# Folding the second layer's first norms into its transform, and writing the head weights once

## The chip, the cores and the metric
The kernel runs on one core of one Trainium2 chip. The metric is device time in microseconds of one execution. Engines are called as in the profile: PE (TensorE, matmuls), PEld (its weight loads), DVE (VectorE), ACT (ScalarE), POOL (GpSimd) and SP (SyncE, which here issues DMAs). SPq and ACTq stand for DMA issues on the queues of SP and ACT.

## What is computed
The input is x of shape (4, 48, 48, 128), in float32: B = 4 images, H = 48 rows, W = 128 columns (the reference calls the axis of 128 the channels) and T = 48 tokens. Two residual layers follow each other:

```python
x = x + _L0_conv_ref(_gn(x), ...)      # a selective scan over the image in four directions
x = x + _L1_conv_ref(_gn(x), ...)      # attention built from Fourier layers

def _gn(v, G=32, eps=1e-5):            # GroupNorm, 32 groups of 4 channels
    m = mean(g, axis=(1, 2, 4)); s = var(g, axis=(1, 2, 4))
    return ((g - m) / sqrt(s + eps)).reshape(v.shape)

def _L1_conv_ref(x, ...):
    xa = x.reshape(B * T, 1, H, W)
    xa_n = _inorm(xa, norm_g[0], norm_b[0])            # per token image: mean and variance over H and W
    k, q = spectral convolution of xa_n to half size + skip, 32 heads
    v    = spectral convolution of xa_n at full size + skip, 32 heads
    attn_w = softmax(q k^T / sqrt(d))                  # 48 x 48 per head and image
    out = attn_w v;  projd = spectral convolution over heads + skip
    attention = _inorm(projd + xa)
    m = two more spectral layers with norms and a gelu
    return _inorm(m) + attention
```

So in the second layer x passes two normalizations at its start: GroupNorm (a scale and a shift for each image and group of the 128 channels), then, per image and token, subtraction of a mean over H and W and multiplication by 1 / sqrt(variance + eps), called r below. The spectral convolutions act on the 2-D Fourier transform of that result.

## The kernel before
`layer0` (up to line 617) is the first layer. Its order on the engines is written out by hand by a helper class; every operation of it is recorded under line 50. It ends when the last image is written to a buffer x1 in device memory, at 4213 us of the profile. Then follows `layer1` (from line 643), in which W lies on the 128 partitions and the free axis is (h, image and token), with BT = B * T = 192. From here up to the last strands the program's operations are put in order by the framework's scheduler, so the order on an engine needn't be that of the text; buffers with few copies (`bufs`) set further limits.

The stages of `layer1` that matter here:

1. *Loads and constants* (656 to 744). x is loaded from x1 into `xa` [128, 48, 192], an image at a time, on SP and ACT in turn (line 744). Each image goes to columns b*48 to b*48+47 of every row h, thus in pieces of 192 bytes in SBUF.
2. *Head weights* (749 to 793). The spectral weights of all heads for V and P are combined into `gw`, transposed (`pgt`, line 789), copied to `gtt`, and written to device memory as `dgt` (line 791), repeated 16 times: the destination is [4, 32, 16, 1152] floats, 2304 KB for each of four k.
3. *Weights in two dimensions* (`spectral_weights`, 948 to 979) for the last two layers. w2 is loaded (ACT queue); a row of it is set to zero; then for each of 2 x 8 blocks POOL makes `wih` (line 971) twice, PE multiplies (`psw`, line 976), ACT copies PSUM to `spw` (line 978, one buffer) and SP stores it to `sp_d` (line 979).
4. *GroupNorm* (990 to 999). For each image and each block of 8 rows ACT copies to a dense block `gblk` (line 992) and DVE takes bn_stats of it (line 993); `group_affine` (620) makes scale and shift, `aff`; four DVE operations apply them to `xa` in place (line 999).
5. *The token norm* (`first_norm`, 695). 48 matmuls with a 128 x 128 matrix of 1/(H*W) (`pm_in`, line 699) sum `xa` over w and h; the mean is subtracted in place on DVE and POOL (`xa`, line 706), ACT squares (`sq`, line 708), 48 more matmuls sum these (`pv_in`, line 710), and r (`in_r`) follows.
6. *Transform along W* (`forward_w`, 721). 48 matmuls `pa_x` (line 729) with `fw` [128, 66]; DVE multiplies by r while it empties PSUM (line 730); SP stores to `da_x` (line 731); `load_a2` (736) reads it back with the axes exchanged, as `a2` [96, 33, 192].
7. *Selections* from `a2` for q and k (`psel`, line 1041), after the transposes of `xa` into `xnt` (lines 1023 and 1026; two tiles of [128, 48, 128], tags p0 and p1). Beside this `prepare` (823) loads small weights, most by SP (lines 893 to 946).
8. *Scores and softmax* (1076 to 1170). They also write `dxt` to device memory, the transformed x.
9. *The head stage* (1216 to 1273). For each of 2 pairs of images, 4 k and 3 q: 16 DMAs on SP fill `xrep` (line 1227, two buffers), each with 16 rows of 4608 bytes from `dxt`. At q = 0 also `grep` (line 1235, four buffers, one per group g of 8 heads): one DMA of 576 KB from `dgt` each. For each of the four g, ACT copies `gp` (1242), DVE forms `v` (1244), POOL `v3` (1248), and PE adds to the accumulators `acc` (1252), with the attention weights as the stationary operand. At the end of each k the sums are emptied, combined and transposed (1258 to 1273).
10. *The last strands* (from 1280): the remaining layers, again in an order written by hand.

`small` and `work` are pools with two buffers for each tag. The tag `blk` in `work` is used by the blocks `a_x` of `forward_w` and by `sq` of `first_norm`. DMAs of SP and of ACT carry one of eight completion semaphores in turn.

Of the kernel before, what the change touches and what calls it, by code (L numbers as in the profile page):

```python
# [10 lines left out]
F32 = mybir.dt.float32  # L11
BF16 = mybir.dt.bfloat16
AF = mybir.ActivationFunctionType
ALU = mybir.AluOpType
# [6 lines left out]
BT = B * T  # L21
# [621 lines left out]
def layer1(ctx, tc, io, x1_dram, out):  # L643
# [17 lines left out]
    def everywhere(name, src, n):  # L661
        return load(name, [128, n], src.partition_broadcast(128), nc.scalar)

    ident = load("ident1", [128, 128], io["c_ident"])
    gmat = load("gmat1", [128, 128], io["c_group"])
    fw = load("fw", [128, 66], io["c_FW"])
    fh = load("fh", [96, 96], io["c_FH"])
    fhi = load("fhi", [96, 96], io["c_FHI"])
    ih = load("ih", [96, 96], io["c_IH"])
    eps = const.tile([128, 1], F32, name="eps1")  # L670
    nc.gpsimd.memset(eps, 1e-5)
    mean_m = const.tile([128, 128], F32, name="mean_m")
    nc.gpsimd.memset(mean_m, 1.0 / (H * W))
    n_g = everywhere("n_g", io["L1_norm_g"], 6)
    n_b = everywhere("n_b", io["L1_norm_b"], 6)
    HB = 8


    turn = [0]

    def either():
        turn[0] += 1
        return nc.gpsimd if turn[0] % 3 == 0 else nc.vector

# [6 lines left out]

    def per_image(t, n=HB):
        return t[:, None, :].to_broadcast([128, n, BT])

    def first_norm(psum, work, x):

        pm = psum.tile([128, 512], F32, tag="st", name="pm_in")
        for q in range(H // 2):
            nc.tensor.matmul(pm[:, 0 : 2 * BT], mean_m, x[:, 2 * q : 2 * q + 2], start=(q == 0), stop=(q == H // 2 - 1))  # L699
        m = small.tile([128, BT], F32, tag="in_m", name="in_m")  # L700
        nc.scalar.copy(m, pm[:, 0:BT])
        nc.vector.tensor_add(m, m, pm[:, BT : 2 * BT])
        pv = psum.tile([128, 512], F32, tag="st", name="pv_in")
        for q in range(0, H, HB):
            d = x[:, q : q + HB]
            either().tensor_sub(d, d, per_image(m))
            sq = work.tile([128, HB, BT], F32, tag="blk", name=f"sq_{q}")
            nc.scalar.activation(sq, d, AF.Square)
            for j in range(0, HB, 2):
                nc.tensor.matmul(  # L710
                    pv[:, 0 : 2 * BT], mean_m, sq[:, j : j + 2], start=(q + j == 0), stop=(q + j == H - 2)
                )
        r = small.tile([128, BT], F32, tag="in_r", name="in_r")
        nc.scalar.copy(r, pv[:, 0:BT])
        nc.vector.tensor_add(r, r, pv[:, BT : 2 * BT])
        nc.scalar.activation(r, r, AF.Sqrt, bias=eps)
        nc.vector.reciprocal(r, r)
        nc.vector.tensor_scalar(r, r, n_g[:, 0:1], None, ALU.mult)
        return r

    def forward_w(psum, work, src, r, name):


        da = dram.tile([2, 33, H, BT], F32, name=f"da_{name}")
        for q in range(0, H, HB):
            a = work.tile([66, HB, BT], F32, tag="blk", name=f"a_{name}{q}")
            for j in range(0, HB, 2):
                p = psum.tile([128, 512], F32, tag="mm", name=f"pa_{name}{q}_{j}")
                nc.tensor.matmul(p[0:66, 0 : 2 * BT], fw, src[:, q + j : q + j + 2], start=True, stop=True)
                nc.vector.tensor_mul(  # L730
                    a[:, j : j + 2], p[0:66, 0 : 2 * BT].rearrange("p (a t) -> p a t", t=BT), per_image(r, 2)[0:66]
                )
            nc.sync.dma_start(da.rearrange("c k h t -> (c k) h t")[:, q : q + HB], a)
        return da

# [5 lines left out]

    xa = img.tile([128, H, BT], F32, name="xa")
    for b in range(B):
        dmas[b % 2].dma_start(xa[:, :, b * T : (b + 1) * T], x1_dram[b])

    pair_t = [img.tile([128, H, 128], F32, tag=f"p{p}", name=f"xnt{p}") for p in range(2)]
    sp_d = [dram.tile([96, 32, 96], F32, name=f"sp_d{i}") for i in range(2)]
# [3 lines left out]
    NC = 384  # L751
    dgt = dram.tile([4, NH, 16, 3 * NC], F32, name="dgt")
    with ExitStack() as pw:
# [30 lines left out]
        for k in range(4):  # L784
            gt = q1.tile([NH, 3, NC], F32, name=f"gtt{k}")
            for c in range(3):
                p = ps_t.tile([128, 512], F32, tag="tr", name=f"pgt{k}_{c}")
                for j in range(3):
                    nc.tensor.transpose(p[0:NH, j * 128 : (j + 1) * 128], gw[:, 3 * k + j, c], ident)
                nc.scalar.copy(gt[:, c], p[0:NH, 0:NC])  # L790
            nc.sync.dma_start(
                dgt[k], gt.rearrange("h c n -> h (c n)")[:, None].to_broadcast([NH, 16, 3 * NC])
            )
    ws_q = everywhere("ws_q", io["wQs"].rearrange("h o -> (h o)"), NH)
# [153 lines left out]
    def spectral_weights(psum, work):  # L948
# [3 lines left out]
        for i, m in enumerate((fh, fhi)):  # L952
# [4 lines left out]
            fht.append(t)  # L957
        none = work.tile([1, 2, 1], F32, tag="none", name="none", bufs=1)
        nc.gpsimd.memset(none, 0.0)
        for n in range(2):  # L960
            w2 = work.tile([96, 2, 32], F32, tag="w2", name=f"w2_{n}", bufs=2)
            for c in range(2):
                for i in range(2):
                    nc.scalar.dma_start(w2[i * 48 : (i + 1) * 48, c], io[f"wM{n}"][c])
            for i in range(2):
                nc.scalar.dma_start(w2[48 * i : 48 * i + 1, :, 0:1], none)
            for k0 in range(0, 32, 4):
                p = psum.tile([128, 512], F32, tag="mm", name=f"psw{n}_{k0}")
                for c in range(2):
                    t = work.tile([96, 4, 96], F32, tag="wih", name=f"wih{n}_{k0}_{c}")  # L970
                    nc.gpsimd.tensor_mul(
                        t,
                        ih[:, None].to_broadcast([96, 4, 96]),
                        w2[:, c, k0 : k0 + 4, None].to_broadcast([96, 4, 96]),
                    )
                    nc.tensor.matmul(p[0:96, 0:384], fht[c], t, start=(c == 0), stop=(c == 1))  # L976
                t = work.tile([96, 4, 96], F32, tag="spw", name=f"spw{n}_{k0}", bufs=1)
                nc.scalar.copy(t, p[0:96, 0:384].rearrange("p (k m) -> p k m", m=96))
                nc.sync.dma_start(sp_d[n][:, k0 : k0 + 4], t)


    with ExitStack() as ph:
# [5 lines left out]
        for b in range(B):  # L988
            st = small.tile([128, 6, 6], F32, tag="st", name=f"st1_{b}")
            for q in range(6):  # L990
                blk = small.tile([128, HB, T], F32, tag="gblk", name=f"gblk{b}_{q}")
                nc.scalar.copy(blk, xa[:, q * HB : (q + 1) * HB, b * T : (b + 1) * T])
                nc.vector.bn_stats(st[:, q], blk.rearrange("p a t -> p (a t)"))
            nc.vector.bn_aggr(mv[:, b], st)
        aff = small.tile([128, 2, B], F32, tag="aff", name="aff1")
        group_affine(nc, small, psst, gmat, eps, mv[:, :, 0], mv[:, :, 1], aff[:, 0], aff[:, 1], B, "l1")
        for b in range(B):
            v = xa[:, :, b * T : (b + 1) * T]
            nc.vector.tensor_scalar(v, v, aff[:, 0, b : b + 1], aff[:, 1, b : b + 1], ALU.mult, ALU.add)
        r0 = first_norm(psst, work, xa)  # L1000
        prepare()
        pl = ph.enter_context(tc.tile_pool(name="l1_plain", bufs=1))
        plain = pl.tile([128, 4, 2, BT], F32, name="plain")


        da = forward_w(psum, work, xa, r0, "x")
        a2 = zp.tile([96, 33, BT], F32, tag="z96", name="a2_x")
        load_a2(a2, da, 33)
        b48 = small.tile([128, 1], F32, tag="b48", name="b48")
        nc.vector.tensor_scalar(b48, n_b[:, 0:1], 1.0 / H, None, ALU.mult)  # L1010
# [5 lines left out]
        for p in range(2):  # L1016
            nc.tensor.matmul(pr[0:96, p : p + 1], r0[0:1, p * 96 : p * 96 + 96], one1, start=True, stop=True)
        nc.scalar.copy(r_t, pr[0:96, 0:2])
        for p in range(2):
            for q in range(0, H, 4):  # L1020
                pt = psum.tile([128, 512], F32, tag="mm", name=f"pxn{p}_{q}")
# [158 lines left out]
    with ExitStack() as ph:  # L1180
# [38 lines left out]
        for pair in range(2):  # L1219
            for k in range(4):  # L1220
                acc = [ps_y.tile([128, 512], F32, tag=f"acc{c}", name=f"acc{pair}_{k}_{c}") for c in range(3)]
                gr = []
                for q in range(3):
# [7 lines left out]
                    for g in range(4):  # L1231
                        t = f"{pair}_{k}_{q}_{g}"
                        if q == 0:
                            r = pg.tile([128, 3, NC], F32, tag="grep", name=f"grep{t}")
                            nc.sync.dma_start(
                                r.rearrange("p c n -> p (c n)"),
                                dgt[k, 8 * g : 8 * g + 8].rearrange("h r n -> (h r) n"),
                            )
                            gr.append(r)
# [592 lines left out]
```

## Time and profile before
| what | value |
|---|---|
| median of three runs | 5088.06 us (5079.85 to 5090.88) |
| the profiled execution's own time | 5084.95 us |
| its span | 5083.1 us |
| last write of x1 issued | 4213.1 us |
| first `psel` matmul | 4390.9 us |
| head stage, first `acc` to last | 4547.8 to 4808 us |
| SP in the head stage | 384 `xrep` issues of 72 KB, 32 `grep` issues of 576 KB |
| head weights written | four stores of 2304 KB |

Times in the profile count from the span's start. "Busy" is the time an engine executes; waiting is not counted. A line of the kind `A <- B: t, n, u` in the waits says that A stood idle for t us in n places until B was done. The chain is followed back from the last instruction to whatever released each step. The span's shares are averages over both layers: the first, with 4213 of the 5083 us, sets PE 83%, DVE 83%, POOL 79% and ACT 57%, and says little about the rest. What lies between 4213 and 4810 has to be read window by window.

### The profile page before, as it was taken

To read this page: it belongs to the slowest core of one execution; us is meant where nothing else is said; L and a number is where in the kernel's file an instruction comes from. 1 tells how busy PE (TensorE), PEld (TensorE's weight loads), DVE (VectorE), ACT (ScalarE), POOL (GpSimd) and SP (SyncE) were. 2 spreads that over 40 slices of the span, in tenths; PEclk is the share of its full clock that TensorE was granted. 3 is DMA by queue.
4 is the path that set the end of the run, shared out by engine and by line. 5 is a ranking of instruction groups with operands and counts; after the bars stand their busy time and mean duration, and the time that the engine had idled before them with its cause. 6 is when DMAs were issued, how large, how long until landed. Compare 5 with 4: busy or idle time off the path is not lost. (4 is left out here: it accounts for less than half of the span.)

```text
span 5083.1 us, 44364 instructions
## 1 busy us (share of the span) xinstructions
PE 4214.9 (83%) x12344; PEld 1897.5 (37%) x12344; DVE 4225.4 (83%) x2908; ACT 2911.3 (57%) x6446; POOL 4033.8 (79%) x2219
## 2 busy tenths in 40 slices
PE   6889898888798988887989888878787785888876
PEld 2334333333343333333433333333333332453343
DVE  3689998989899989898999898999999983356536
ACT  3666566666565666665656666656656552223334
POOL 4589998988899989798999898899999872346531
PEclk9989999999899999998999999999899986989977
DMA  1223233323233333232333332333233226236546
GB/s 54 72 88 101 93 113 92 101 91 96 93 107 105 104 93 100 88 99 92 106 103 107 91 102 84 99 105 103 99 104 94 93 71 127 64 81 176 166 99 152
DMA packets 276767, 509.25 MB, mean 100 GB/s; under 512 B 100602, under 2 KB 185434, under 8 KB 276326
## 3 DMA queue, kind: packets, MB, share of 16 engines
q1 hardware_dynamic: 265318, 502.61, 32.8%
q10 hardware_dynamic: 11200, 3.81, 0.5%
q8 instruction: 97, 1.59, 0.1%
q14 instruction: 152, 1.25, 0.1%
HBM read 462.58 MB, written 43.72 MB: 100 GB/s over the span
## 5 line engine op out<-in xcount | busy, mean ns | idle before, releaser
L50 POOL TENSOR_TENSOR hc<-h,cbc 128x960 f32<-128x960 f32 (+1 forms) x1280 | 2719.2, 2140 | 461.9 <-DVE h L50 337.4
L50 DVE TENSOR_TENSOR_SCAN h<-da,carry,db 128x961 f32<-128x961 f32 (+1 forms) x1280 | 2702.3, 2130 | 121.2 <-ACT carry L50 86.8
L50 ACT ACTIVATE da<-dt,a_neg 128x480 f32<-128x480 f32 (+1 forms) x2560 | 1661.2, 649 | 1247.4 <-DVE h L50 1201.6
L50 PE MATMUL yp<-hc,ident 128*128 128x480 f32 (+1 forms) x5120 | 2279.6, 573 | 6.8 <-POOL hc L50 6.6
L50 PEld LDWEIGHTS yp<-hc,ident 128*128 128x128 f32 x5120 | 1008.0, 199 | 1428.5 <-issue 1022.4
L50 DVE TENSOR_TENSOR db<-du,pb 128x960 f32<-128x960 f32 (+1 forms) x960 | 1063.1, 1107 | 210.6 <-PE pb L50 155.5
L50 PE MATMUL pb<-bs,pick 112*128 112x480 bf16 (+1 forms) x960 | 360.6, 376 | 400.9 <-DVE db L50 399.2
L50 POOL TENSOR_TENSOR db<-du,bbc 128x960 f32<-128x960 f32 (+1 forms) x320 | 688.5, 2152 | 0.0
L50 PE MATMUL pc<-pad,cdiag 128*128 128x480 f32 (+1 forms) x630 | 283.2, 561 | 9.0 <-ACT pad L50 9.0
L1248 POOL TENSOR_TENSOR v<-grep,xrep 128x768 f32<-128x768 f32 x96 | 174.2, 1821 | 111.2 <-PE acc L1252 64.0
L50 POOL TENSOR_TENSOR du<-dt,xc 128x480 f32<-128x480 f32 (+1 forms) x160 | 204.9, 1281 | 37.1 <-ACT dt L50 37.1
L1252 PE MATMUL acc<-v,attn_c 128*64 128x384 f32 x1152 | 212.8, 511 | 25.8 <-POOL v L1248 15.8
L1244 DVE TENSOR_TENSOR v<-gp,xrep 128x1536 f32<-128x1536 f32 x96 | 165.3, 1754 | 82.4 <-PE acc L1252 36.2
L50 PE MATMUL px<-xc,w_xp 128*112 128x480 f32 (+1 forms) x320 | 215.6, 761 | 17.0 <-ACT xc L50 13.3
L50 ACT COPY db<-carry 128x1 f32<-128x1 f32 x1280 | 226.0, 177 | 5.4 <-DVE db L50 2.1
L50 PEld LDWEIGHTS <-pick 112*128 112x128 bf16 x960 | 97.9, 102 | 331.8 <-issue 307.6
L50 ACT ACT_TABLE_LOAD x146 | 187.3, 1283 | 25.5 <-PE gv_g L50 13.8
L50 PE MATMUL pd<-xd,w_dt 8*128 8x480 f32 (+1 forms) x320 | 167.9, 605 | 38.6 <-ACT bs L50 24.6
L50 ACT COPY carry<-h 128x2 f32<-128x2 f32 x1024 | 192.7, 188 | 0.0
L50 PEld LDWEIGHTS pc<-pad,cdiag 128*128 128x128 f32 x630 | 121.9, 194 | 142.3 <-issue 114.8
L50 PE MATMUL yp<-y,ident 128*128 128x480 f32 (+1 forms) x240 | 166.4, 823 | 0.2
L1252 PEld LDWEIGHTS acc<-v,attn_c 128*64 128x64 f32 x1152 | 88.2, 141 | 146.6 <-issue 63.4
(367 smaller groups left out, 3183.2 us busy)
## 6 DMA issues: line engine op xcount, KB each, us to landing
cbc<-cd SPq DMA_DIRECT2D x512, 480.0 KB
bbc<-cd SPq DMA_DIRECT2D x256, 240.0 KB
cbc<-cd SPq DMA_DIRECT2D x128, 384.0 KB
xrep<-dxt SPq DMA_DIRECT2D x384, 72.0 KB
grep<-dgt SPq DMA_DIRECT2D x32, 576.0 KB
bbc<-cd SPq DMA_DIRECT2D x64, 192.0 KB
dgt<-gtt SPq DMA_DIRECT2D x4, 2304.0 KB
x<-in_xT SPq DMA_DIRECT2D x16, 288.0 KB
```

The source lines that it names most:

```text
L50: return lambda *args, **kw: self._tc.keep_in_program_order(emit(*args, **kw))
L1244: nc.vector.tensor_mul(v, gp[:, None, :, 0:NC].to_broadcast([128, 2, 2, NC]), x[:, :, 0:2])
L1248: nc.gpsimd.tensor_mul(v3, r[:, 2:3].to_broadcast([128, 2, NC]), x[:, :, 2])
L1252: nc.tensor.matmul(acc[c][64 * b : 64 * b + 64, 0:NC], attn_c[:, 2 * pair + b, g, q], v[:, b, c] if c < 2 else v3[:, b], start=first, stop ...
```

## The change
In the second layer:

- x is loaded image by image into two tiles `x_in` (dense, two images each), on the tags p0 and p1 that `xnt` uses later. The loads stand ahead of those of `gmat`, `fw` and the head weights; the eight loads of w2 stand ahead of them and are held in constants.
- bn_stats reads `x_in`; the copies to `gblk` are gone. The affine isn't applied to x any more. Its scale multiplies `fw` (`fwa`, one for each image), its shift comes as a bias `fwb` when PSUM is emptied, half on DVE and half on ACT.
- The mean over H and W is summed from `x_in` by 24 matmuls with the scale as weights, image b into partitions 32b to 32b+31 (four column groups); a helper `spread` reduces over h and distributes it to all partitions by small matmuls. The variance is summed the same way. Centring (DVE, from `x_in` into `xa`) and squares (ACT) take one image and 8 rows at a time, 24 operations each.
- The transform doesn't contain mean and r: the mean is taken out of `a2` at frequency 0 (`p0_x`), and `a2` is multiplied by r there, in three DVE operations. `forward_w` and the variance pass are generators that run in turns, and `da_x` is stored on ACT's queue.
- `spectral_weights` sets the row to zero by a multiplication; `wih` is made on POOL for c = 0 and on DVE for c = 1; `spw` has two buffers, and `sp_d` is stored on ACT's queue.
- `dgt` is written once (144 KB for each k), and `grep` is read with eight DMAs of 72 KB, each of which reads one head's row for 16 partitions.

The diff, cut to its core:

```diff
+    x_in = [img.tile([128, 2, H, T], F32, tag=f"p{p}", name=f"x_in{p}") for p in range(2)]
+    for b in range(B):
+        dmas[b % 2].dma_start(x_in[b // 2][:, b % 2], x1_dram[b])
-    xa = img.tile([128, H, BT], F32, name="xa")
-    for b in range(B):
-        dmas[b % 2].dma_start(xa[:, :, b * T : (b + 1) * T], x1_dram[b])
...
     def first_norm
-        for q in range(H // 2):
-            nc.tensor.matmul(pm[:, 0 : 2 * BT], mean_m, x[:, 2 * q : 2 * q + 2], ...)
+        nc.vector.tensor_scalar(a_m, aff[:, 0], 1.0 / (H * W), None, ALU.mult)
+        def sums(p, what, weight):
+            for q in range(0, H, HB):
+                for b in range(B):
+                    nc.tensor.matmul(p[32 * b : 32 * b + 32, 0 : HB * T], weight(b), what(b, q), ...)
+        def spread(p, name, more=False):
+            nc.vector.tensor_reduce(v, p[:, 0 : HB * T].rearrange("p (h t) -> p t h", t=T), AX.X, ALU.add)
+            for b in range(B):
+                nc.tensor.matmul(ob, g_of[:, b], v, start=True, stop=not more)
+                if more:
+                    nc.tensor.matmul(ob, aff[:, 1, b : b + 1].to_broadcast([128, 128]), over_w, ...)
...
-            either().tensor_sub(d, d, per_image(m))
-            nc.scalar.activation(sq, d, AF.Square)
-            for j in range(0, HB, 2):
-                nc.tensor.matmul(pv[:, 0 : 2 * BT], mean_m, sq[:, j : j + 2], ...)
+            for b in range(B):
+                nc.vector.scalar_tensor_tensor(d, x[b // 2][:, b % 2, q : q + HB], aff[:, 0, b : b + 1],
+                    m[:, b, None, :].to_broadcast([128, HB, T]), ALU.mult, ALU.add)
+                nc.scalar.activation(sq[:, b], d, AF.Square)
+                nc.tensor.matmul(pv[32 * b : 32 * b + 32, 0 : HB * T], mean_m, sq[:, b], ...)
+            yield
...
     def forward_w
+            nc.vector.tensor_scalar(fwa[:, b], fw, aff[:, 0, b : b + 1], None, ALU.mult)
+        nc.tensor.matmul(pb[0:66, 0:B], fw, aff[:, 1], start=True, stop=True)
-                nc.tensor.matmul(p[0:66, 0 : 2 * BT], fw, src[:, q + j : q + j + 2], ...)
-                nc.vector.tensor_mul(a[:, j : j + 2], p[0:66, 0 : 2 * BT]..., per_image(r, 2)[0:66])
-            nc.sync.dma_start(da...[:, q : q + HB], a)
+                nc.tensor.matmul(p[0:66, 0 : HB * T], fwa[:, b], x[b // 2][:, b % 2, q : q + HB], ...)
+                if b % 2:
+                    nc.scalar.activation(o, v, AF.Identity, bias=fwb[:, b : b + 1])
+                else:
+                    nc.vector.tensor_scalar(o, v, fwb[:, b : b + 1], None, ALU.add)
+            nc.scalar.dma_start(da...[:, q : q + HB], a)
+            yield
...
-    dgt = dram.tile([4, NH, 16, 3 * NC], F32, name="dgt")
+    dgt = dram.tile([4, NH, 3 * NC], F32, name="dgt")
-            nc.sync.dma_start(dgt[k], gt...[:, None].to_broadcast([NH, 16, 3 * NC]))
+            nc.sync.dma_start(dgt[k], gt.rearrange("h c n -> h (c n)"))
...
     def spectral_weights
-                    nc.gpsimd.tensor_mul(t, ih..., w2[:, c, k0 : k0 + 4, None]...)
+                    (nc.gpsimd, nc.vector)[c].tensor_mul(t, ih..., w2[:, c, k0 : k0 + 4, None]...)
-                t = work.tile([96, 4, 96], F32, tag="spw", name=f"spw{n}_{k0}", bufs=1)
+                t = work.tile([96, 4, 96], F32, tag="spw", name=f"spw{n}_{k0}", bufs=2)
-                nc.sync.dma_start(sp_d[n][:, k0 : k0 + 4], t)
+                nc.scalar.dma_start(sp_d[n][:, k0 : k0 + 4], t)
...
-                blk = small.tile([128, HB, T], F32, tag="gblk", name=f"gblk{b}_{q}")
-                nc.scalar.copy(blk, xa[:, q * HB : (q + 1) * HB, b * T : (b + 1) * T])
-                nc.vector.bn_stats(st[:, q], blk.rearrange("p a t -> p (a t)"))
+                v = x_in[b // 2][:, b % 2, q * HB : (q + 1) * HB]
+                nc.vector.bn_stats(st[:, q], v.rearrange("p h t -> p (h t)"))
-        for b in range(B):
-            v = xa[:, :, b * T : (b + 1) * T]
-            nc.vector.tensor_scalar(v, v, aff[:, 0, b : b + 1], aff[:, 1, b : b + 1], ALU.mult, ALU.add)
-        r0 = first_norm(psst, work, xa)
+        norm = first_norm(psst, work, x_in, aff, xa)
+        trans = forward_w(psum, work, x_in, aff, "x")
+        next(norm)
+        for _ in range(6):
+            next(trans)
+            next(norm)
+        da = next(trans)
+        r0 = next(norm)
...
+        nc.tensor.matmul(p0[0:H, 0:BT], over_h, a2[0:H, 0], start=True, stop=True)
+        nc.vector.tensor_sub(a2[0:H, 0], a2[0:H, 0], p0[0:H, 0:BT])
+        for s in range(0, 33, 11):
+            v = a2[:, s : s + 11]
+            nc.vector.tensor_mul(v, v, r0[0:96, None, :].to_broadcast([96, 11, BT]))
...
-                            nc.sync.dma_start(r..., dgt[k, 8 * g : 8 * g + 8].rearrange("h r n -> (h r) n"))
+                            for i in range(8):
+                                nc.sync.dma_start(r[16 * i : 16 * i + 16]..., dgt[k, 8 * g + i].partition_broadcast(16))
```

## The prediction, made before the changed kernel ran
> **What bounds the kernel now.** I read the windows first, stage by stage, because the page's shares are dominated by the first layer, which the change doesn't touch (its last line is at 4213 us). The columns are the window, its length, busy PE, PEld, DVE, ACT and POOL with instruction counts, granted TensorE clock, DMA share and GB/s.
> ```profile
> 4206.00:4230.00 24.00, 6.65 (x11) 2.74 (x10) 5.40 (x13) 0.00 (x0) 11.95 (x64) 0.57 0.77 146
> 4256.00:4290.00 34.00, 24.55 (x64) 12.56 (x62) 8.40 (x14) 2.26 (x4) 5.56 (x7) 0.79 0.98 201
> 4316.00:4346.00 30.00, 23.27 (x50) 8.17 (x49) 2.79 (x8) 5.88 (x14) 17.81 (x22) 0.80 0.22 62
> 4547.00:4810.00 263.00, 222.24 (x1213) 94.55 (x1212) 174.96 (x118) 84.80 (x117) 170.61 (x94) 0.96 0.57 164
> ```
> From 4206 to 4391 no engine is full and the limiter changes every 30 us; in the head stage (last row) PE leads, with DMA at 164 GB/s. Next the chain of waits between 4205 and 4400 (start, duration, what):
> ```profile
> 4219.79 22.39 DMA xa<-x
> ...
> 4266.30 5.66 DVE xa L999 x4
> 4272.01 18.12 PE pm_in L699 x48
> 4290.89 6.67 DVE xa L706 x2
> 4297.58 1.49 ACT sq L708
> 4299.12 13.18 PE pv_in L710 x40
> ...
> 4316.77 1.87 DMA sp_d<-spw
> 4318.72 0.48 ACT spw L978
> 4319.22 1.88 DMA sp_d<-spw
> ```
> The pair sp_d/spw repeats up to 4346: one spw buffer, so each round is a 0.48 copy and a 1.87 store, and about 30 us go to it while PE holds the following pa_x behind psw. Last, SP's own queue in the head stage (timeline: start, us, line, how many):
> ```profile
> 4538.27 33.33 SPq L1227 DMA_DIRECT2D xrep<-dxt  x48
> 4571.70 1.78 SPq L1235 DMA_DIRECT2D grep<-dgt  x4
> 4573.57 29.26 SPq L1227 DMA_DIRECT2D xrep<-dxt  x48
> 4602.95 2.78 SPq L1235 DMA_DIRECT2D grep<-dgt  x4
> 4605.84 29.52 SPq L1227 DMA_DIRECT2D xrep<-dxt  x48
> ```
> One (pair, k) is 48 + 4 issues; eight of them run from 4538 to 4808, 33.5 us each. The waits view has beside it:
> ```profile
> POOL v L1248 <- DMA xrep<-dxt: 33.4, 8, 18.4
> DVE v L1244 <- DMA xrep<-dxt: 29.7, 9, 7.1
> ```
> so v already waits for xrep eight or nine times, once per k. Taken one by one, issues that queue without a wait start every 0.463 us (0.42 busy and a gap), xrep like grep; the 16-way broadcasts of mask and wpv ahead of them have the same 0.42 and 0.47, so an eighth of the bytes will not be issued faster.
>
> **What the Trainium skill says.** "DMA: Bandwidth & Descriptors", section "Issuing engines are not separate DMA queues", holds that issuing from another engine saves sequencer time and adds no bandwidth: the trace agrees that here the sequencer is the scarce part (0.463 us an issue, while DMA is 57% busy). "TensorEngine Tiling (Array Packing)", Key Properties, says that narrow tiles run side by side and that a change of tile mode drains TensorE; psel at L1041, in four groups of 32 columns, agrees with the first half (163 matmuls of 0.329 us are busy 8.0 us together); the second is shown by no stretch of this trace. "SBUF — State Buffer", section "SBUF: two separate sides", describes a port pair that VectorE and GpSimd lock against each other: L706 takes 4.98 us on POOL and up to 5.01 on DVE against 1.76 undisturbed.
>
> **The change part by part, up to psel** (it starts at 4390.9 now).
> *Load of x.* 3072-byte packets become 9216-byte ones. xrep's 4608-byte packets at 251 ns give 16 x 4608 / 251 = 294 GB/s; 4.72 MB then need 16 us, so x lands near 4236 rather than 4242: 6 gained (0 to 8). The eight small w2 loads now ahead of it run during the first layer's tail.
> *Statistics.* Now 24 copies (0.51 us, ACT) and 24 bn_stats (0.55, DVE) alternate, and bn_stats are kept back by head-weight work; the affine factors come at 4266.3, 24 us after the load. Between the last aggregate (4257.7) and gm_l (4262.4) PE ran psw; that goes. After the last image: 6 x 0.55 + 0.3 + group affine (2 matmul pairs, 1.28 table load, seven small DVE operations: 4.0 + 0.3) plus 1.74 of d_qk and a wQ load that stand in front, 12.5 us: 4248.7. The four affines of 1.47 (5.66 on the chain) are gone. So pm_in may start at 4249 instead of 4272: 23 gained.
> *Means.* 24 matmuls of 384 columns instead of 48. But the scheduled order puts nine of them first and the other fifteen one to one between the 32 psw, which now all precede pa_x. Per k0 two psw and one pm, 3 x 0.65 = 1.95 us; 4249 + 9 x 0.5 + 16 x 1.95 + about 3 of mode changes = 4288. The psw/spw rounds no longer limit (two buffers: (0.48 + 1.9 + 0.3) / 2 = 1.3 a round). That uses up most of the 23 gained (pm_in ended at 4290.1), but psw's 30 us between pr and pa_x vanish.
> *Variance and transform, interleaved.* The blk tag has two buffers, and the order a, sq, a, sq gives a always the same one: a round is 1.2 of evacuation plus the da_x store (3.46 and 3.75 in the chain), 4.8; six rounds 29 us. The engines need less per round: DVE 4 x 0.55 centring (estimate from 128x384 rows) + 2 x 0.55, 3.3; ACT 4 x 0.45 + 2 x 0.5 + one issue, 3.3; PE 8 x 0.65 at most, 5.2, if column groups don't overlap. End 4317; r0, which follows pv, is by then ready. Now centring, squares, pv, psw and pa_x take 4290 to 4367.
> *Spectrum.* p0_x needs the first piece of a2 (load now 8.26 for all, first piece about 3): 4320. xnt's 24 evacuations of 0.683 then take 16.4: psel near 4337 to 4338. The three products with r0 (2.4 each, an estimate: v's 1.76 for 1536 columns, scaled to 2112) end near 4332 and are covered by xnt; without that cover they cost 7.2.
> Sum: 4390.9 - 4338 = **53 us gained**. Bounds: 42 (PE at half clock through a third of the psw loop, 10 more) to 60 (column groups overlap, load at full rate). The single dgt store (576 KB in all in place of 9.4 MB between 4247 and 4294) frees DMA, which nothing above waits for.
>
> **Between psel and the head stage** PE, ACT, DVE and POOL have the same order as before; no change.
>
> **Head stage.** xrep's 48 issues per (pair, k) stay; grep's four become 32 of 72 KB. All on SP: 80 x 0.463 = 37.0 us for each k, where the period is 33.5. So SP, which had 52 x 0.463 = 24.1 us of work and slack, becomes the bound: at least 8 x 3.5 = 28 lost. It doesn't reach this floor, since xrep has two buffers and SP is in order. Once v of (k, 1) has freed a buffer, SP issues 16 for (k+1, 0), then 32 grep, then 16 for (k+1, 1): 64 x 0.463 = 29.6, landing about 2.3 later, then the four v (8.1, PE's acc being 2.2 a group) before the next buffer is free: 40.0 a period, +6.5. Counted the same way the present kernel gives (16 + 4 + 16) x 0.463 + 2.3 + 8.1 = 27, which isn't binding, and PE sets 33.5. Behind the grep run wait (k+1, 1)'s xrep, thus v on DVE and POOL, thus acc on PE, which idles about 6 us a period and may fall to the lower clock (acc 3.6 to 3.9 instead of 2.2), up to 1.7 more. Seven periods x 6.5 (to 7.9) + 7 for the first k: 52 (52 to 62); if part of a grep run is absorbed in slack, the floor of 28. I take **54 lost**. At a pitch of 0.42 (the busy time of an issue alone) the same sum gives 64 x 0.42 + 10.4 = 37.3, 3.8 x 7 + 4 = 31; at 0.36 (the median of grep's 32 present issues, most of which had waited first) 33.4: nothing lost.
>
> **Sum.** -53 + 54 = +1 on 5084.95 (the span of 5083.1 and 1.9 around it). The profile lies 3.1 below the median of the runs, so +1 on 5088.06: **5089**. The tail strands after the head move as a block.
>
> **Rivals.**
> *Head transfers stay hidden.* For: DMA moves 164 GB/s with room, grep's present issues show a median of 0.36 us, and four grep buffers let early ones go ahead. Against: back-to-back issues show 0.463 without exception in shape. Pays from a pitch near 0.40 downward; then -53 + 0 to 20: about 5044 (5033 to 5068).
> *SP's queue outweighs the front (the slower side).* Place: the 32 grep issues between the xrep of (k+1, 0) and (k+1, 1). Price 6.5 a period as above plus the lower clock, 7.9, and PE's restart at every step: up to 66, against a front gain of 42: +15 to +30, about 5110. Decides from a pitch of 0.463 with the lower clock in every k, or a front gain under 45.
> *The front gives less.* psw and pm_in at the lower clock need 3.85 us a k0, +30, and mode changes add; gain 25: 5088 - 25 + 54 = 5117. For: window 4230 to 4256 shows a clock of 0.57. Against: the loop is dense and the clock is 0.79 to 0.9 once PE is busy. I count it with the previous one.
> That the edits don't do what they say: the grep tiles are the same bytes, and the order of issues shows 256 in place of 32, so no.
>
> **How the numbers follow.** Balance (5074 to 5102): 0.46. Transfers hidden: 0.27. SP outweighs or the front gives less: 0.27. 0.2%, about 10 us, is what can be told from no change. In the balance case a quarter each lies beyond 10 us on either side, so faster 0.27 + 0.11 = 0.38, slower 0.27 + 0.12 = 0.39, the rest 0.23. For 8 in 10 the range must reach well into both outer cases: 5048 to 5118; the likeliest one's own is 5074 to 5102.
>
> **What would show it.** Right: psel starting 53 us earlier; no stretch of sp_d/spw pairs; in the head stage SP rows of 32 grep of about 15 us each, a period near 40, v waiting for xrep 6 us more per k, PE busy down from 85% to 72%. Wrong: a period near 33.5 (pitch below 0.40), or psel gaining under 42 with psw or da_x stores on the chain.

## The result and the profile after
The changed kernel takes 5127.2 us (median of four runs; 5124.6 to 5133.5) against 5086.8 beside it. The ratio on record is 1.0092, 95% interval 1.0079 to 1.0104; the two medians alone give 1.0079. It is 40 us slower by the medians, outside the range that was given (5048 to 5118).

The two profiled executions (spans 5083.1 and 5126.9) divide into four stretches. The times are those of the first `psel` matmul and of the first and last `acc` matmul in each trace:

| stretch | before | after | difference |
|---|---|---|---|
| start to first `psel` | 4390.8 | 4350.0 | -40.8 |
| first `psel` to first `acc` | 156.9 | 156.9 | 0 |
| first to last `acc` (the head stage) | 260.8 | 347.8 | +87.0 |
| last `acc` to the end | 274.6 | 272.3 | -2.3 |

So the front did gain, 41 instead of 53, and the head stage lost 87 instead of 54. The timeline of SP's queue in the head stage of the changed kernel (start, us, line, number of issues):

```profile
4511.72 29.50 SPq L1296 DMA_DIRECT2D xrep<-dxt  x48
4541.32 15.32 SPq L1305 DMA_DIRECT2D grep<-dgt  x32
4556.90 29.62 SPq L1296 DMA_DIRECT2D xrep<-dxt  x48
4586.63 14.69 SPq L1305 DMA_DIRECT2D grep<-dgt  x32
```

Between two runs of grep lie 45.3 us here; the eight ends of k are 44.4 apart on the mean, and were 33.5 apart before. POOL in the same k (timeline: start, us of the group, line, and in brackets the idle time ahead of it and what ended it):

```profile
4548.28 1.81 POOL L1318 TENSOR_TENSOR v<-grep,xrep 128x768 f32<-128x768 f32 x1 [6.19 <-DMA grep<-dgt]
4552.42 1.81 POOL L1318 TENSOR_TENSOR v<-grep,xrep 128x768 f32<-128x768 f32 x1 [2.34 <-DMA grep<-dgt]
4556.53 1.81 POOL L1318 TENSOR_TENSOR v<-grep,xrep 128x768 f32<-128x768 f32 x1 [2.30 <-DMA grep<-dgt]
4560.64 1.81 POOL L1318 TENSOR_TENSOR v<-grep,xrep 128x768 f32<-128x768 f32 x1 [2.30 <-DMA xrep<-dxt]
4568.91 3.58 POOL L1318 TENSOR_TENSOR v<-grep,xrep 128x768 f32<-128x768 f32 x2 [6.45 <-DMA xrep<-dxt]
```

The four v of (k, 0) come 4.1 us apart, each held by a landing (eight issues at 0.463 would be 3.7), and v of (k, 1) then waits for the xrep issued behind the last grep. Afterwards (4568.9 to 4587) POOL and PE are busy with v of (k, 1) and (k, 2) until the next run of grep. The windows show the same as an average (length, busy PE, PEld, DVE, ACT and POOL, granted clock, DMA share, GB/s): the second row is the stretch with the grep run, the third the end of the k.

```profile
4507.00:4855.00 348.00, 240.62 (x1208) 96.40 (x1208) 178.46 (x118) 86.74 (x119) 172.45 (x95) 0.85 0.72 129
4541.00:4570.00 29.00, 15.05 (x76) 5.23 (x72) 10.49 (x9) 6.17 (x9) 9.41 (x6) 0.84 1.04 147
4578.00:4587.00 9.00, 8.91 (x56) 4.09 (x54) 7.18 (x5) 2.41 (x3) 7.94 (x5) 1.00 0.44 123
```

PE is busy 69% of the stage (240.6 of 348) where it was 85%. One thing in the second row was not in the prediction: DMA is full (1.04) at only 147 GB/s. The first window below is of the kernel before while grep was loaded, where 290 GB/s passed at a share of 0.94. The other two are of the changed kernel, when xrep alone goes out, just before the grep run and 8 us after it:

```profile
4671.30:4676.20 4.90, 4.90 (x29) 2.89 (x27) 3.15 (x2) 0.00 (x0) 3.72 (x3) 0.85 0.94 290
4536.00:4540.00 4.00, 4.00 (x24) 2.05 (x24) 2.86 (x3) 0.80 (x1) 3.50 (x2) 1.00 0.52 152
4565.00:4573.00 8.00, 2.23 (x8) 1.07 (x10) 3.42 (x2) 1.47 (x2) 3.58 (x2) 0.66 1.04 154
```

The same DMAs pass at the same rate with a share of 0.52 and of 1.04, so a full share alone doesn't show that 147 GB/s is a limit. But SP's queue also waits for landings in the head stage (waiting line, what ended the wait: us in total, times, longest):

```profile
SPq L1296 <- DMA xrep<-dxt: 11.6, 60, 0.4
SPq L1296 <- DMA grep<-dgt: 5.7, 31, 0.2
SPq L1305 <- DMA grep<-dgt: 3.6, 19, 0.3
```

These are 20.9 us, 2.6 for each k. So besides SP's issues there is a second suspect, the transfers themselves, and the experiments had to separate the two.

In the front, the chain of waits of the changed kernel:

```profile
4266.23 1.46 PE psw L1032 x4
4267.69 0.76 PE pm_in L716 x2
4268.45 1.46 PE psw L1032 x4
...
4304.55 3.46 DMA da_x<-a_x
...
4326.05 12.56 DMA a_x<-da_x
4338.73 1.03 DVE a_x L1075
```

The pairs of spw and sp_d are gone. Every 2.22 us PE issues two psw and one pm_in (1.46 + 0.76; each of these float32 matmuls has two records), and nothing else holds the loop. Behind it two da_x stores stand on the chain, this one and one of 4.17 us at 4315.2.

### The profile page after: what moved, and what is told of

Read it like the earlier page. It is cut to its first block, busy times and chain, and to the rows that moved or that the text cites. A ratio compares the mean times of both kernels' runs of the same rounds, so it can differ in the third digit from the quotient of the medians.

```text
span 5126.9 us, 44853 instructions
## 1 busy us (share of the span) xinstructions
PE 4209.6 (82%) x12372; PEld 1882.8 (37%) x12372; DVE 4229.5 (82%) x2945; ACT 2910.8 (57%) x6451; POOL 4011.9 (78%) x2207
## 5 line engine op out<-in xcount | busy, mean ns | idle before, releaser
L1322 PE MATMUL acc<-v,attn_c 128*64 128x384 f32 x1152 | 230.3, 552 | 93.5 <-POOL v L1318 90.9
L1312 ACT COPY gp<-grep 128x768 f32<-128x768 f32 x96 | 76.5, 803 | 193.9 <-DVE v L1314 120.3
```

The lines of the kernel that those rows point to most:

```text
L1312: nc.scalar.copy(gp[:, :, 0:NC], r[:, 0:2])
L1322: nc.tensor.matmul(acc[c][64 * b : 64 * b + 64, 0:NC], attn_c[:, 2 * pair + b, g, q], v[:, b, c] if c < 2 else v3[:, b], start=first, stop ...
```

## The experiments
All ratios are to the kernel before, timed beside it. "Period" is the mean distance of the eight ends of k (the copies of the first accumulator). Period and first `psel` come from the one profiled execution of each kernel.

| kernel | ratio (95% interval) | first `psel` | period |
|---|---|---|---|
| before | 1 | 4390.8 | 33.5 |
| changed | 1.0092 (1.0079 to 1.0104) | 4350.0 | 44.4 |
| head_undone | 1.0001 (0.9992 to 1.0010) | 4388.0 | 33.9 |
| one_issue | 1.0110 (1.0094 to 1.0125) | 4353.2 | 45.3 |
| eight_rep | 1.0171 (1.0156 to 1.0187) | 4392.6 | 44.9 |
| grep_act | 1.0199 (1.0184 to 1.0214) | 4352.5 | 50.8 |
| two_copies | 0.9988 (0.9980 to 0.9996) | 4353.9 | 37.0 |
| wide_8 | 1.0163 (1.0148 to 1.0178) | 4355.6 | 49.2 |
| before_two | 1.0030 (1.0018 to 1.0041) | 4374.5 | 39.0 |
| blk_apart | 0.9982 (0.9975 to 0.9988) | 4351.1 | 37.9 |
| issues_only | 1.0166 (1.0149 to 1.0184) | 4386.0 | 44.2 |
| four_copies | 0.9938 (0.9923 to 0.9953) | 4352.0 | 33.7 |
| four_psw | 0.9911 (0.9896 to 0.9925) | 4345.3 | 33.5 |
| late_16 | 1.0022 (1.0015 to 1.0029) | 4356.2 | 32.9 |

**head_undone**: the changed kernel with the head weights as before.

```diff
+    dgt = dram.tile([4, NH, 16, 3 * NC], F32, name="dgt")
+            nc.sync.dma_start(dgt[k], gt...[:, None].to_broadcast([NH, 16, 3 * NC]))
+                            nc.sync.dma_start(r..., dgt[k, 8 * g : 8 * g + 8].rearrange("h r n -> (h r) n"))
```

> The changed kernel with its head stage as before: dgt written 16 times, grep read by one DMA of 576 KB for each g. Theory A (the 32 grep issues on SP stand between two fills of xrep and lengthen every k): the head's period falls from 44.6 to 33.5 us, 8 x 11 = 88 us, so 5127 - 88 = about 5040 and a ratio to the kernel before of 0.991; psel starts where it does in the changed kernel (4350) or up to 4 us later, since 9.4 MB more are written. Theory C (the front of the layer is what lost, and its gain of 41 us is given back before the head stage): no less than 5085.

Measured: 5084.5, the time of the kernel before. The head's period is back to 33.9, but psel is back too, at 4388.0. The theory was right about the head and wrong about the front: 38 of the front's 41 us go with the store of dgt. SP's timeline and the chain of this kernel show how.

```profile
4241.17 63.80 SPq L852 DMA_DIRECT2D dgt<-gtt  x4
4307.73 34.82 SPq L954 DMA_DIRECT2D w_wK<-in_wK  x7
...
4347.95 4.36 SPq L960 DMA_DIRECT2D w_wK<-in_wK  x15
...
4365.49 0.33 SPq L806 DMA_DIRECT2D a_x<-da_x  x1
```

```profile
4267.84 11.46 DMA sp_d<-spw
...
4297.43 10.28 DMA da_x<-a_x
...
4309.63 11.83 DMA da_x<-a_x
...
4342.71 27.63 issue
4370.34 0.86 PE p_x L1073 x2
```

Four stores of 2304 KB occupy SP from 4241 to 4305. The stores of sp_d and da_x, 1.9 and 3.5 us otherwise, take 10 to 12 us beside them. Then the small weight loads, which stand behind dgt on SP, are late, and SP's part of the load of a2 stands behind these: it starts at 4365.5, against 4325.4 in the changed kernel. The chain has 27.6 us of "issue" up to 4370.3, in which the profile names nothing that PE waits for; that queue fits it. Whether the bytes of the store or its place on SP's queue cost more was not separated.

**one_issue**: dgt written once, one DMA for each grep that repeats each head's row 16 times.

```diff
-                            for i in range(8):
-                                nc.sync.dma_start(r[16 * i : 16 * i + 16]..., dgt[k, 8 * g + i].partition_broadcast(16))
+                            nc.sync.dma_start(r..., dgt[k, 8 * g : 8 * g + 8][:, None].to_broadcast([8, 16, 3 * NC]))
```

> The changed kernel, dgt written once, but grep read by one DMA for each g whose source repeats each head's row 16 times (32 issues in all, the same bytes read from the same rows as in the changed kernel). Theory A (issues): period 33.5, about 5040, like the kernel with the head undone. Theory B (16 partitions that read the same 4608 bytes are slow as a transfer, which also makes the landing of 4.3 us): v still waits for grep, the period stays at 40 or more, 5095 to 5127.

Measured: 5139.6 and a period of 45.3, with 32 grep issues in all. It was a miss for theory A as the only cause. In the k of the window below, POOL's v of (k, 0) come 4.1 to 4.7 us apart, each waiting for its grep: 576 KB (590 thousand bytes) in 4.65 us, 127 GB/s. Columns as above:

```profile
4589.00:4607.00 18.00, 9.10 (x36) 3.75 (x38) 5.65 (x4) 3.36 (x5) 5.42 (x3) 0.62 0.58 137
```

DMA is slow while it is hardly more than half busy (a share of 0.58). That agrees with the Trainium skill, "DMA: Bandwidth & Descriptors", section "Why a DMA increments its semaphore by 16 and not by 1", which says that a DMA goes to as many engines, at most 16, as divide the slowest dimension of both its access patterns: 8 rows lead here, so 8 engines of the 16. The slow landings hold xrep too. The wait of SP's queue for grep in the head stage (us in total, times, longest):

```profile
SPq L1296 <- DMA grep<-dgt: 112.3, 29, 4.7
```

In this k SP issues four grep and four xrep, and the next four xrep go out only 4.1 to 4.8 us apart (4593.9, 4598.7, 4603.4, 4607.5), as the greps land. That fits the eight semaphores that SP's DMAs carry in turn: the ninth DMA waits for the first. So this run takes the issues away and puts landings in their place, at the same point of the queue. It doesn't show what the changed kernel would do if its issues were free.

**eight_rep**: dgt repeated 16 times, grep still read by eight DMAs.

```diff
+    dgt = dram.tile([4, NH, 16, 3 * NC], F32, name="dgt")
-                                    dgt[k, 8 * g + i].partition_broadcast(16),
+                                    dgt[k, 8 * g + i],
```

> The changed kernel, with dgt written 16 times as before, but grep still read with eight DMAs of 72 KB, each of 16 different rows. Theory A (issues): the 256 issues remain, so 5127 within 6 us, period 44 to 45. Theory B (reads of one row by 16 partitions): these are gone, so the period falls by a good part, to 34 to 40, 5045 to 5090.

Measured: 5169.5. The period stays at 44.9, so reading one row 16 times isn't what makes the changed kernel's head slow. (The other 42 us are the front: psel at 4392.6, about as in head_undone.) The transfers are as slow as there with 16 different rows: DMA share 1.04 at 141 GB/s in the grep run.

**grep_act**: the changed kernel's 256 grep DMAs on ACT's queue.

```diff
-                                nc.sync.dma_start(
+                                nc.scalar.dma_start(
                                     r[16 * i : 16 * i + 16]..., dgt[k, 8 * g + i].partition_broadcast(16),
```

> The changed kernel with grep's 256 DMAs issued on ACT's queue instead of SP's; all transfers are the same. Theory A (SP's queue): SP is back to 48 issues a period; ACT has 9.6 us of gp copies and 32 x 0.46 = 15 us of issues in a period of 33.5 and holds them, though gp of one k stands behind grep issues that wait for a buffer; 5040 to 5065. Theory B (transfers): no change, 5115 to 5130.

Measured: 5187.1, period 50.8, slower than on SP. ACT's timeline:

```profile
4613.40 0.80 ACT L1312 COPY gp<-grep 128x768 f32<-128x768 f32 x1 [0.77 <-DMA grep<-dgt]
4613.43 5.63 ACTq L1305 DMA_DIRECT2D grep<-dgt  x8
4621.76 0.80 ACT L1312 COPY gp<-grep 128x768 f32<-128x768 f32 x1 [7.55 <-DMA grep<-dgt]
4621.77 6.85 ACTq L1305 DMA_DIRECT2D grep<-dgt  x8
4630.48 0.80 ACT L1312 COPY gp<-grep 128x768 f32<-128x768 f32 x1 [7.92 <-DMA grep<-dgt]
```

gp of one group stands between the issues of the next: the copy waits for its grep to land, and the next eight issues wait for the copy. One group costs 8.4 to 8.7 us in place of 4.1. That is a chain of its own, so this run doesn't decide between issues and transfers.

**two_copies**: dgt written twice, so that 16 rows stand at the head of the source.

```diff
+    dgt = dram.tile([4, NH, 2, 3 * NC], F32, name="dgt")
+                            nc.sync.dma_start(r..., dgt[k, 8 * g : 8 * g + 8].rearrange("h r n -> (h r) n")[:, None]
+                                .to_broadcast([16, 8, 3 * NC]))
```

> The changed kernel, dgt written in two copies (288 KB for each k), grep read by one DMA for each g whose source is 16 rows (8 heads times 2 copies), each repeated 8 times. Theory D (what is slow is not the number of issues but how a DMA spreads: eight rows at its head keep it on 8 DMA engines[...]): now [...]grep's packets return to about 180 ns, the head period to 33.5, and psel stays near 4351: about 5042, ratio 0.992. Theory B (reads of one row by several packets are slow whatever the spread): the period stays over 40, 5100 to 5135.

Measured: 5074.4; psel 4353.9, period 37.0. Neither theory's number. The windows of a grep load in this kernel and in four_copies (below):

```profile
4612.00:4621.00 9.00, 3.70 (x20) 1.56 (x19) 4.84 (x5) 3.26 (x5) 4.34 (x3) 0.82 1.02 231
```

```profile
4606.00:4612.00 6.00, 4.58 (x31) 2.37 (x28) 3.29 (x4) 0.48 (x1) 4.12 (x4) 1.00 0.95 337
```

With DMA full in both, 231 GB/s pass with two copies and 337 with four. So repeated reading of the same rows does slow a large transfer (the median packet of 4608 bytes takes 322 ns in the window with two copies, 178 in the one with four, and 178 in the kernel before with sixteen). The wait of SP's queue for grep follows suit, here in two_copies and in four_copies:

```profile
SPq L1298 <- DMA grep<-dgt: 55.1, 25, 3.2
SPq L1298 <- DMA grep<-dgt: 25.2, 15, 2.8
```

In the kernel before it is 24.7 us.

**wide_8**: two copies, each grep cut into eight DMAs of 144 columns over all partitions.

```diff
+                            for i in range(8):
+                                nc.sync.dma_start(r...[:, 144 * i : 144 * i + 144],
+                                    dgt[...][:, None, 144 * i : 144 * i + 144].to_broadcast([16, 8, 144]))
```

> As the kernel with two copies, but each grep cut in eight DMAs of 144 columns over all 128 partitions: 256 issues of 72 KB again, now with wide targets. Theory A alone (SP's issues, 0.463 us each): 64 issues in the chain, 29.6 + 2.3 + 8.1 = 40 a period, 5084 + 0 to 10. Theory D alone (transfers): the period returns to 33.5 and the time to 5040 to 5060. If both must be paid as in the changed kernel: 5127.

Measured: 5164.8, period 49.2. A run of 32 such issues takes at least 20.4 us, 0.64 each instead of 0.463, so the run is not the clean test that was meant. With its own pitch the chain of the prediction gives 7.4 + 20.4 + 7.4 + 2.3 + 8.1 = 45.6, 3.6 less than measured.

**before_two**: the kernel before, with dgt and grep of two_copies only.

> The kernel before with only the head weights changed: dgt in two copies, grep by one DMA for each g as in the kernel with two copies. Theory E (the front's gain is a joint one: both the new front and the small store are needed; the 16-fold store keeps SP's queue and the DMA engines, but the kernel before then waits for its chain of spw and sp_d and for the norm anyway): psel from 4391 to 4380 to 4388, 5075 to 5083. Theory F (the store alone held the front; the other edits are worth little): psel near 4355, about 5045.

Measured: 5096.0, with psel at 4374.5, between the two theories. The small store alone gives the old front 16 us, the new front alone (head_undone) gives 3, both give 37 (two_copies) to 41. The gain is joint. The total is no better than before, since grep with two copies costs 41 us in the head stage (301.5 us from first to last acc, against 260.8).

**blk_apart**: two_copies with a tag of its own for the squares.

```diff
-            sq = work.tile([128, B, HB, T], F32, tag="blk", name=f"sq_{q}")
+            sq = work.tile([128, B, HB, T], F32, tag="sq", name=f"sq_{q}")
```

> The kernel with two copies, and the squares on a tag of their own, so that a_x and sq have two buffers each. The rounds of a_x and sq from 4289 to 4325 took 36 us where 29 had been reckoned. If the shared blk buffers make them (a evacuation waits for the store of a_x two blocks back): 6 to 10 us less than the kernel with two copies. If the engines or the da_x stores do: within 3 us of it.

Measured: 5072.4, psel 2.8 us earlier: by the number, within the bound for "not the buffers". The trace says otherwise of the rounds themselves: from the first da_x store to the last they take 21.5 us (4296.3 to 4317.8) instead of 26.7 (4296.6 to 4323.3), so the shared buffers did make them longer. psel gets little of it, because SP, in another order here, is at the small weight loads until 4324 and sends three of its four a2 loads only from 4332.9 on (from 4326.9 with two copies).

**issues_only**: head_undone, with seven tiny DMAs behind each of its four grep DMAs, into a tile that nothing reads.

```diff
+                            for i in range(7):
+                                j = 4 * (((pair * 4 + k) * 4 + g) * 7 + i)
+                                nc.sync.dma_start(junk[:, j : j + 4], dgt[k, 8 * g + i, 0, 0:4].partition_broadcast(16))
```

> The kernel with the head undone (16 copies, one grep DMA for each g) with seven more DMAs behind each grep, of 16 bytes for each of 16 partitions, into a tile that nothing reads: 32 issues for grep again, and hardly a byte more to move. It is compared with the kernel with the head undone (5084, period 33.4). Theory A (issues in the chain xrep, grep run, xrep): 29.6 + 2.3 + 8.1 = 40.0 a period, up to 41.7, so 5084 + 8 x 6.6 to 8.3 = 5137 to 5151. Theory D (only the transfers): period 33.5, 5084 to 5090.

Measured: 5164.5 against 5084.5 for head_undone, 80 us for 224 issues that move 57 KB together. The period is 44.2. SP's timeline:

```profile
4588.55 0.34 SPq L1307 DMA_DIRECT2D grep<-dgt  x1
4588.93 3.20 SPq L1313 DMA_DIRECT2D junk<-dgt  x7
4592.39 28.24 SPq L1299 DMA_DIRECT2D xrep<-dxt  x48
4620.73 0.35 SPq L1307 DMA_DIRECT2D grep<-dgt  x1
```

and POOL's:

```profile
4592.48 1.81 POOL L1325 TENSOR_TENSOR v<-grep,xrep 128x768 f32<-128x768 f32 x1 [2.03 <-DMA grep<-dgt]
4602.45 3.59 POOL L1325 TENSOR_TENSOR v<-grep,xrep 128x768 f32<-128x768 f32 x2 [8.16 <-DMA xrep<-dxt]
4608.62 1.82 POOL L1325 TENSOR_TENSOR v<-grep,xrep 128x768 f32<-128x768 f32 x1 [2.58 <-PE acc L1329]
```

Seven issues in 3.20 us are 0.46 each although they carry 256 bytes. The grep run ends, xrep of (k, 1) goes out, and v starts after 8.2 us without work (6.5 in the changed kernel). The period is longer than even theory A had it (40.0 to 41.7). So issues that carry almost nothing are enough for the changed kernel's longer period. That its transfers cost nothing isn't shown by this: 32 x 72 KB at 147 GB/s are 16.0 us (an estimate), as long as the 15.3 of the issues, and the two run at the same time. No run has the changed kernel's transfers without its issues.

**four_copies**: as two_copies, with `4` copies and a source of [32, 4, 3 * NC].

> As the kernel with two copies, with four (576 KB written for each k, grep's source 32 rows repeated 4 times). If the repeated reading of one row is what keeps grep at 225 GB/s and 330 ns a packet (two copies; 16 copies: 178 ns): packets of 220 to 270 ns, period 34 to 35 in place of 36.0, so 8 to 16 us off in the head stage, and 1 to 4 us on in the front for the larger store: 5060 to 5070. If the number of copies is nothing to it: 5074 to 5078.

Measured: 5050.7. The period is 33.7, psel 4352.0: 38.8 of the front's 40.8 without the loss of the head. That is better than expected; SP waits for grep as little as in the kernel before (25.2 us against 24.7).

**four_psw**: four_copies, with the weights in two dimensions behind the variance pass.

```diff
-        spectral_weights(psum, work)
         mv = small.tile([128, B, 2], F32, tag="mv", name="mv1")
...
         r0 = next(norm)
+        spectral_weights(psum, work)
         prepare()
```

> The kernel with four copies, and the weights in two dimensions (psw and its stores) put behind the variance pass. In the changed kernel 15 of the 24 pm_in matmuls stand singly between psw at 0.76 us each, where four together take 0.85. If that and the wait for a2 (5 us before p0_x, which psw now fills) are real costs of the front: psel 10 to 14 us earlier than with four copies, and the time too. If psw only moves: within 3 us of it.

Measured: 5037.7, 13 us less than four_copies, but psel comes only 6.7 earlier, between the two expectations. Another 4.5 lie between psel and the first acc (156.9 against 161.4); their cause is open. The order on PE in the changed kernel and in this one:

```profile
4257.27 1.53 PE L1032 MATMUL psw<-wih,fht 96*96 96x384 f32 x4
4258.73 0.83 PE L716 MATMUL pm_in<-x_in,a_m 128*32 128x384 f32 x2
4259.49 1.53 PE L1032 MATMUL psw<-wih,fht 96*96 96x384 f32 x4
```

```profile
4251.64 4.33 PE L716 MATMUL pm_in<-x_in,a_m 128*32 128x384 f32 x46
```

The 24 pm_in of the program leave 48 records, two each. Singly, one pm_in takes 0.76 us; here 23 of them, four column groups side by side, take 4.33, or 0.19 each. psw now stands behind the variance pass (4292 to 4325), where the chain has 4.8 us of wih on POOL and a store of sp_d of 5.9, which gives part of it back.

**late_16**: dgt written once, copied to 16 copies in device memory beside the scores.

```diff
                     nc.sync.dma_start(dxt[b, k], xt.rearrange("r c n -> r (c n)"))
+                    if b == 0:
+                        nc.sync.dma_start(dgt16[k], dgt[k][:, None].to_broadcast([NH, 16, 3 * NC]))
```

> The changed kernel, dgt written once in the front and copied 16-fold from device memory to device memory beside the scores, where DMA is 13 to 16% busy; grep as in the kernel before. If the front's gain needs only that the 9.4 MB stay out of it, and the head needs 16 copies: psel near 4355 (one of the four copies is issued ahead of the a2 load), period 33.5, 5045 to 5055. If the copies collide with dxt's stores in the scores, these get longer by their waits: 5060 to 5090.

Measured: 5093.7, above both expectations. psel (4356.2) and the period (32.9) came as wanted, but the first acc came 193 us after psel instead of 157: six dxt stores go out between 4501 and 4537, after the scores, and xrep needs them. Whether the copies held them by their traffic or the scheduler by another order was not separated.

## Why the prediction was wrong
Two terms of its sum were off. The head's loss was put at 54 and was 87; the front's gain was put at 53 and was 41. The first is the larger, and it is the step that failed: the period with 32 grep issues was mis-sized. One sentence on dgt was also wrong in kind. Of the signs that the prediction had named for being right, the grep runs of about 15 us, the vanished pairs of sp_d and spw and PE's fall (69%; 72% forecast) came. The period near 40 and the 53 us of psel did not.

*The period of the head.* The prediction's step was "64 x 0.463 = 29.6, landing about 2.3 later, then the four v (8.1 ...): 40.0 a period". issues_only shows the same chain, with hardly a byte more to move than in head_undone. Its terms there, between 4576.5 and 4620.7, are: grep run 15.9 (14.8 assumed; the first issue of some groups waits for its buffer), xrep of (k, 1) 7.3 (7.4), landing to the first v 2.8 (2.3), four v until the next buffer is free 9.6 (8.1), xrep of (k+1, 0) 8.6 (7.4). Together 44.2 instead of 40.0. Of the 4.2 missing, 2.2 are in the 64 issues, which aren't gapless (31.8 instead of 29.6), 1.5 in v, whose third waits 2.6 for PE, and 0.5 in the landing. In the k of the changed kernel shown above, between 4541.3 and 4586.6, the same terms are 15.6, 8.1, 3.9, 9.8 and 8.0, together 45.3: the issues 2.0 more than the prediction's, v 1.7 and the landing 1.6. Its period is 44.4 on the mean, 10.95 more than before, where 6.5 had been forecast. Seven periods x 10.95 + 10.3 in the first k make 87; 54 had been taken. The low end of the bounds, 28, was far off: no slack absorbed anything. So the mechanism was right, and the sizes of its terms were not. How much of the 10.95 the transfers would make by themselves stays open.

*The pitch.* 0.463 us, whatever the size: right for xrep and grep in the changed kernel (the median of their issues) and for 256-byte DMAs. Not every DMA on SP has it: the small weight loads of head_undone, shown above, start every 0.29 us (15 in 4.36).

*"The single dgt store ... frees DMA, which nothing above waits for."* This step was wrong in kind. Without it the new front reaches psel 38 us later. The sum of 53 was built from edits that, by themselves, give 3. With the 16-fold store in place the same waits return as longer da_x and sp_d stores and a late a2. As the changed kernel has the small store too, the error did no harm to the forecast of the front: that is luck, not a right account.

*The front's size*, 41 for 53. aff came at 4250.5 (4248.7 assumed), the psw loop's end at 4289 (4288), both about right. In the loop, errors cancel: a k0 took 2.22 us, not 1.95, and the 3 us put down for changes of tile mode don't show as time of their own. The rounds of a and sq took 36 us, to 4325.4, not 29. The six da_x stores went out 5.5 us apart on the mean where 4.8 had been taken, and the first only 5 us behind the psw loop. blk_apart shows that the shared buffers are in this. PE was busy 31.2 of 35 us there, and the prediction's own upper figure for it was as much (six rounds of 5.2), so the 29 lay below what it had allowed PE. The a2 load was misread: the 8.26 in the chain is the stretch of one wait, while the load ran from its first issue on SP at 4371.1 to 4385 when PE went on, 14 us. Its first piece took 5.0, not 3, in the changed kernel; xnt began at 4332.9 instead of 4320. The prediction had named this outcome as a sign of being wrong, "psel gaining under 42 with psw or da_x stores on the chain": 40.8, with 7.6 us of da_x stores on it.

*Between psel and the head* nothing changed, as forecast: 156.9 us in both.

*The rivals.* The slower one, SP's queue outweighing the front, is what happened, at a price of 87 against 41, more than its "up to 66" against 42. One of its two marks held, a front gain under 45. Its other was the lower clock: the granted clock was 0.85 in the head stage against 0.96 before, and acc took 552 ns on the mean against 511, but whether that lengthened the period was not tried. The faster one, hidden transfers, would have needed a pitch near 0.40 or below, and no run showed one below 0.46 for grep or xrep on SP's queue.

## What to carry to other kernels
When one large DMA is split into many, price the issues by the queue's pitch and place them in the chain of buffers: with 32 issues of 0.46 us between two refills of a double buffer a turn took 11 us longer here, although the queue as a whole had only 37 us of work in 44. Then ask what the queue itself waits for: with one slow DMA in place of eight it stood 112 us in the head stage until grep had landed, and the turn was as long. Replicating data in device memory is a trade in both directions; between 1 copy (slow to spread) and 16 (9.4 MB that crowd out others), 4 copies and one DMA took hardly any of either loss, and with psw moved the kernel runs at 0.9911 of the time before. And before crediting a gain to an edit, ask which other edit it needs: undo one part at a time.

## What was not expected of the hardware
- An issue of a DMA into 16 partitions on SP takes 0.46 us for 256 bytes as for 72 KB; one over 128 partitions with repeated rows takes 0.63 to 0.68 (0.64 in wide_8 and two_copies, 0.68 in one_issue), and without repeated rows 0.47 (grep in the kernel before).
- The rate of a 576 KB load depends on how its source is laid out, with the same bytes arriving at the same place: 127 GB/s (8 rows, each repeated 16 times), 231 (16 rows, 8 times), 337 (32 rows, 4 times), 290 with 128 rows in the window of the kernel before.
- DMAs that fill 16 partitions each run at 141 to 147 GB/s when DMA is full, with 16 different rows (eight_rep) as with one row 16 times (the changed kernel). xrep's, which fill 16 partitions too, pass at 152 GB/s with a share of 0.52 ahead of a grep run. What makes the packets longer, and which end of the transfer it is, was not tried.
